# A two-layer decoder on one core: rotary tables of later batches made early and kept in DRAM, key preparation and query scaling at other places

## The chip, the core and the metric

The kernel runs on one core of a Trainium2 chip. The metric is device time in microseconds (us) of one execution. The core has five engines with in-order queues of their own: TensorE (PE in the profile, its weight loads PEld), VectorE (DVE), ScalarE (ACT), GpSimd (POOL) and SyncE (SP), which issues most of the DMAs here. L12 means line 12 of the kernel before.

## The reference

Four batches of 256 tokens, width 256, go through a decoder of two layers. Only the part around the change is shown in code; the rest is told in a sentence each.

```python
# layer 0: self-attention (16 heads, causal), attention over ctx (1601 tokens, masked), ternary feed-forward
x = x + _L0_attn_ref(_layernorm(x), ...)
x = x + _L0_xattn_ref(_layernorm(x), ctx_2048, mask)
x = x + _L0_ffn_ref(_layernorm(x), w_fc, w_proj)
# layer 1: gated recurrence, then the grouped attention that the change is about, then 8 experts, top 2
x = x + _L1_attn_ref(_layernorm(x), ...)
x = x + _L1_xattn_ref(_layernorm(x), ctx_2048, Wq, Wk, Wv, Wo, q_norm_w, k_norm_w, ctx_pos, tok_pos)
x = x + _L1_ffn_ref(_layernorm(x), w_gate, wi_0, wi_1, wo)

def _L1_xattn_ref(draft_hidden, context_hidden, ...):      # 16 query heads, 4 key heads, head size 128
    q = _rms_norm(draft_hidden @ Wq.T, q_norm_w)
    kv_in = concatenate([context_hidden, draft_hidden], axis=1)      # 1601 + 256 = 1857 keys
    k = _rms_norm(kv_in @ Wk.T, k_norm_w)
    v = kv_in @ Wv.T
    q, k = _rope(q, draft_pos), _rope(k, all_pos)      # x * cos(emb) + rotate_half(x) * sin(emb)
    probs = softmax(q @ k.T / sqrt(128))
    return (probs @ v) @ Wo.T
```

The positions differ from batch to batch, so the rotary tables are computed on the chip: angles (position times frequency, brought into the range of the Sin function), then cos and sin multiplied by the norm weights, for 1857 key positions (15 chunks of 128, `ctabk` and `stabk`, 128x1920 each) and for 256 query positions (`ctabq` and `stabq`, 128x256 each).

## The kernel before, in words

Everything is float32. The kernel has two parts that overlap a little.

**The front** (to about 525 us). Four generators, one for each batch, run the stages of layer 0 and the recurrence of layer 1 (`before`: `self_attention`, `memory_attention`, `feed_forward`, `recurrence`). A loop over ticks advances them in turn; batch b starts at tick `START[b]`. Beside them other generators are advanced as filler: `values_ahead` (the values of layer 1's attention, computed for whole batches and kept in DRAM, tiles `vah`, `vst`), `keys_ahead` (the unrotated keys of batch 3, kept in DRAM), `shared_weights` (the ternary weights, from tick `TERN`), and `before_head` (what the first head of the long stage needs, from tick `SIDE`). The order in which the program issues instructions on each engine is made by a scheduler from this order of emission; `behind` adds that a piece isn't placed ahead of what was emitted before it.

**The long stage** (about 525 to 1690 us): layer 1's attention. The 16 units of batch and key head are called heads here, each with 4 query heads in two pairs. `steps` runs over 8 steps for each pair. A step emits, in this order: the exponential of an older pair's score tile (subtraction of the maximum `bc` on VectorE, L1383; Exp on ScalarE, L1386; the running sum on POOL, L1398), one score tile of two key chunks (`bsc` on TensorE, L1361; its scaled copy on ScalarE, L1362; the running maximum `acc` on VectorE, L1366), and two key chunks of an older pair's weighted values (`bpo`, L1407). After a pair, `maximum` turns `acc` into `bc` by transposes (`tm`, `mq`, `bc`), and `finish` multiplies by the output weights (`bpw`, L1437).

Between these stand pieces for the next head, at places that are written out by hand: place 2s comes after the scores of step s and place 2s + 1 after its weighted values, so a place is half a step. `base` is the first place of the head before. Each piece is a generator with stops in it:

- `prep_q` (two for each head, j = 0, 1): projection `pq` (L1239), squares on ScalarE (L1189), products with the tables on VectorE (`ropeq`, `ropuq`, L1190 and L1191), their sum (L1196) and the root of the mean square (`rnq`, L1199) on POOL; stop; scaling of the four heads by it on ScalarE (L1203); stop; transposes `tpq` and the copy to `qTb`. The stops are `HB` and `HC` places after the projection.
- `prep_kv` (units 0 to 3, up to 4 key chunks each): load of the context (`cTk`), projection `pk` (L1290), the same rotation, its root `kn` (which later scales the scores' copies); stop; transposes `tpk` and the copy to `kTb` (L1303). Unit i makes key chunks 4i to 4i + 3; unit 0 holds the batch's own tokens too.
- `angles` (9 pieces) and `tables`, once for each batch, `tokens` (the layer norm of the batch's tokens: `normed_tokens` with a root by POOL's power, L272) and `experts` of the batch before (`mo`: another such root), all spread over the places.

The first call of `tiles(b, g)` for a head takes its buffers and issues the loads of its key weights and of the kept values `vb`. The score tiles and most other TensorE results go through one ring of PSUM banks (`p1`), so a result that is copied late holds a bank. Rotary tables have one buffer each.

```python
    QA, KA, HB, HC = (2, 6), (11, 13, 15, 17), 5, 8
            for f, when in ((prep_q, QA), (prep_kv, KA)):
                for i, o in enumerate(when):
                    gen = f(b, g, i)
                    spot = put(base + 2 * o, gen, bank=f is prep_q)
                    if f is prep_q:
                        put(spot + HB, gen)
                    put(spot + HC, gen, True, True)
```

Of the kernel before, what the change touches and what calls it, by code (L numbers as in the profile page):

```python
# [33 lines left out]
NROPE = 3  # L34
TERN = 34
SIDE = 48
KEPT = 3
# [79 lines left out]
def decoder_kernel(ctx: ExitStack, tc: tile.TileContext, at, t, out):  # L117
# [861 lines left out]
    def experts(b):  # L979
# [12 lines left out]
        yield  # L992
        r1 = rsqrt(mv[:, :, 1], 1e-5, f"mo{b}")
        yield
# [120 lines left out]
    def angles(b):  # L1115
# [3 lines left out]
        nc.sync.dma_start(out=pi, in_=t["pos"][b])  # L1119
        if b == 0:  # L1120
            V.tensor_scalar(knw, knw, math.sqrt(HD1), None, ALU.mult)
        pf = wk.tile([P, NCH], F32, tag="pf", name=f"pf{b}")
# [25 lines left out]
    def tables(b, only="kq"):  # L1148
# [3 lines left out]
        for nm, n, w in (("k", NCH, knw), ("q", 2, qnw)):  # L1152
# [13 lines left out]
            yield  # L1166

    def normed_tokens(b):
        mv = moments(xs[b], f"xb{b}")
        r1 = rsqrt(mv[:, :, 1], 1e-5, f"xb{b}")  # L1170
        bt[b]["centred"] = lambda: centred(fa(0, f"bxh{b}"), xs[b], mv, r1)
# [33 lines left out]
    def tiles(b, g):  # L1205

        if (b, g) not in gt:
            gt[b, g] = {

                "kT": odd("w3", f"kTb{b}{g}") if g % 2 else wk.tile([P, NKEY], F32, tag="kT", name=f"kTb{b}{g}"),  # L1210
                "v": (
                    odd("w4", f"vb{b}{g}")[:, 0 : NCH * HD1] if g % 2 else wk.tile([P, NCH * HD1], F32, tag="v", name=f"vb{b}{g}")
                ).rearrange("p (c d) -> p c d", c=NCH),
                "kn": sm([P, NCH], f"kn{g % 2}", f"kn{b}{g}", 1),
                "wkv": weight(
                    wk.tile([P, 512], F32, tag="wkv", name=f"wkv{b}{g}", bufs=2), "wkv1", 0, D, g * 256, (g + 1) * 256
                ),
            }
            for i in range(4):
                if (b, i) in kept_values:  # L1220
                    n, w = units(i)
                    r = min(P, w)
                    nc.sync.dma_start(
                        out=gt[b, g]["v"][0:r, 4 * i + 2 : 4 * i + 2 + n, :],
                        in_=kept_values[b, i][:, 0:r, g * HD1 : (g + 1) * HD1].rearrange("c p n -> p c n"),
                    )
        return gt[b, g]

    def prep_q(b, g, j):
# [75 lines left out]
    def before_head(b, g):  # L1305

        if g == 0:
            if b == 0:
                yield from angles(b)
            yield from tables(b)  # L1310
        late = None
        for i in (1, 2, 3):
# [141 lines left out]

    QA, KA, HB, HC = (2, 6), (11, 13, 15, 17), 5, 8
    DE, DW = 10, 11
# [36 lines left out]
    for k, (b, g) in enumerate(heads):  # L1493
        base = 32 * (k - 1)
        if k:
            if g == 0:
                gen = angles(b)
                for i in range(9):
                    put(base - 81 + 6 * i, gen, i == 8)
                gen = tokens(b)  # L1500
                for i, o in enumerate((-8, -6, -3)):
                    put(base + o, gen, i == 2, i == 2)
                for o, n in ((-5, "q"), (-3, "q"), (7, "k"), (11, "k")):
                    gen = tables(b, n) if o in (-5, 7) else gen
                    put(base + o, gen, o in (-3, 11))
            for f, when in ((prep_q, QA), (prep_kv, KA)):
                for i, o in enumerate(when):
                    gen = f(b, g, i)
                    spot = put(base + 2 * o, gen, bank=f is prep_q)
                    if f is prep_q:  # L1510
                        put(spot + HB, gen)
                    put(spot + HC, gen, True, True)
        gen = loader(b, g)
# [43 lines left out]
    tern = shared_weights()  # L1557
    keys = keys_ahead()
    gens = [before(b) for b in range(B)]
    work = steps()  # L1560
    through, tick, step, said = [False] * B, 0, 0, None
    while not all(through):
# [18 lines left out]
        if tick >= TERN:  # L1581
            behind(tern)
        if through[0] and psb:
            if said != "first":
# [85 lines left out]
```

## Time and profile before

| | us |
|---|---|
| median of 3 runs | 1748.08 |
| lowest and highest | 1747.93, 1750.08 |
| the profiled execution's own time | 1749.43 |
| its span, first to last instruction | 1747.4 |
| mean granted clock of TensorE | 0.993 |

| engine | busy us | share | instructions |
|---|---|---|---|
| PE | 1694.9 | 97% | 6642 |
| PEld | 971.5 | 56% | 6642 |
| DVE | 1302.7 | 75% | 2429 |
| ACT | 997.4 | 57% | 1742 |
| POOL | 877.5 | 50% | 719 |

The page is one execution, taken by the hardware profiler. Matmuls are pipelined and their ends are modelled, so a busy PE is not PE at its peak. A group is told by its line, engine, operation and tiles (out<-in) with its count, its busy time and the mean duration of one in ns; behind that stands the idle time of the engine just before it and what ended most of it. A list of waits names who waited for whom (total, times, longest). A timeline gives start, duration and, in brackets, the idle time before. A table of stretches gives the busy time of each engine between two times, the granted clock of TensorE, and what the DMAs moved.

### The profile page before, as it was taken

The numbers are of one execution on the slowest core, as the hardware profiler recorded it, in microseconds if no ns is written. First come the engines' busy times: TensorE is split into PE (matmuls) and PEld (weight loads), VectorE is DVE, ScalarE is ACT, GpSimd is POOL, SyncE is SP. The second block draws the span as 40 slices with busy tenths as digits, with TensorE's granted clock in tenths as the row PEclk, the third lists the DMA queues.
The fourth block names the chain that finished last, engine by engine and source line by source line (L and its number), as shares of the span: only waits on it lengthen the run. The fifth ranks groups of instructions, "written<-read, shape, count | busy, mean of one in ns | idle before, by whom it ended". The sixth has DMA issues, their size and how long they took to land.

```text
span 1747.4 us, 20643 instructions
## 1 busy us (share of the span) xinstructions
PE 1694.9 (97%) x6642; PEld 971.5 (56%) x6642; DVE 1302.7 (75%) x2429; ACT 997.4 (57%) x1742; POOL 877.5 (50%) x719
## 2 busy tenths in 40 slices
PE   8899989999999999999999999999999999999998
PEld 4455668765555455554555555555555555445546
DVE  6653476787668777787877878777877878788776
ACT  3456653656456656566665656556565656656551
POOL 2210032211126576676766756655665776676651
PEclk9999999999999999999999999999999999999999
DMA  7221334212231121121212121121222113011102
GB/s 258 99 90 50 90 99 128 75 66 90 97 109 46 38 82 35 55 58 31 89 32 70 47 67 52 55 82 35 73 61 67 51 37 93 26 37 48 43 0 67
DMA packets 113554, 119.10 MB, mean 68 GB/s; under 512 B 10000, under 2 KB 87332, under 8 KB 113448
## 3 DMA queue, kind: packets, MB, share of 16 engines
q1 hardware_dynamic: 111624, 116.39, 21.6%
q10 hardware_dynamic: 1824, 1.41, 0.3%
q8 instruction: 53, 0.87, 0.2%
q14 instruction: 53, 0.43, 0.1%
HBM read 100.20 MB, written 17.57 MB: 67 GB/s over the span
## 4 chain that ended last, share of the span: by engine, by line
PE 64%; DVE 12%; POOL 9%; ACT 9%; issue 4%; DMA 1%; POOLq 0%; DVEq 0%; ACTq 0%
PE bpo L1407 17%; PE bsc L1361 16%; PE pk L1290 5%; POOL sum L1398 5%; PE mph L1053 2%; PE bpw L1437 2%; PE vah L355 2%; ACT s L1386 2%; ACT s L1362 2%; DVE acc L1366 1%; PE xpo L740 1%; DVE s L1383 1%; PE pq L1239 1%; POOL ropeq L1196 1%; PE xsc L695 1%
## 5 line engine op out<-in xcount | busy, mean ns | idle before, releaser
L1398 POOL TENSOR_TENSOR sum<-sum,s 128x512 f32<-128x512 f32 (+1 forms) x411 | 536.7, 1306 | 84.1 <-ACT s L1386 59.0
L1361 PE MATMUL bsc<-qTb,kTb 128*128 128x512 f32 (+1 forms) x960 | 459.5, 599 | 6.8 <-ACT kTb L1303 6.7
L1407 PE MATMUL bpo<-s,vb 128*128 128x512 f32 (+1 forms) x960 | 459.9, 598 | 0.4 <-ACT s L1386 0.4
L1362 ACT ACTIVATE s<-bsc,kn 128x512 f32<-128x512 f32 (+1 forms) x480 | 316.5, 683 | 211.6 <-PE bsc L1361 194.6
L1366 DVE SCALAR_TENSOR_TENSOR acc<-bsc,kn,acc 128x512 f32<-128x512 f32 x448 | 333.0, 743 | 89.2 <-ACT s L1362 73.3
L1383 DVE TENSOR_TENSOR s<-s,bc 128x1024 f32<-128x1024 f32 (+1 forms) x256 | 289.4, 1142 | 14.7 <-PE bc L1379 14.5
L1386 ACT ACTIVATE s<-s 128x1024 f32<-128x1024 f32 (+1 forms) x256 | 256.5, 1006 | 53.8 <-DVE s L1383 52.2
L1361 PEld LDWEIGHTS bsc<-qTb,kTb 128*128 128x128 f32 (+1 forms) x960 | 174.2, 188 | 191.9 <-issue 135.3
L1407 PEld LDWEIGHTS bpo<-s,vb 128*128 128x128 f32 (+1 forms) x960 | 169.8, 191 | 141.7 <-issue 137.9
L1389 POOL TENSOR_TENSOR sum<-s 128x512 f32<-128x512 f32 x32 | 40.8, 1276 | 198.6 <-ACT s L1386 198.6
L1196 POOL TENSOR_TENSOR ropek<-ropek,ropuk 128x512 f32<-128x512 f32 (+1 forms) x64 | 78.2, 1222 | 123.7 <-DVE ropuk L1191 122.4
L1203 ACT ACTIVATE ropeq<-ropeq,rnq 128x128 f32<-128x128 f32 x128 | 41.2, 390 | 110.7 <-POOL rnq L1199 107.1
L355 PE MATMUL vah<-wv,vcT 128*128 128x512 f32 (+1 forms) x156 | 77.7, 633 | 5.1 <-DMA vcT<-in_ctxT 3.1
L1290 PEld LDWEIGHTS pk<-wkv,cTk 128*128 128x128 f32 x624 | 76.3, 192 | 8.3 <-issue 4.5
L1290 PE MATMUL pk<-wkv,cTk 128*128 128x128 f32 x624 | 77.4, 275 | 0.0
L1199 POOL TENSOR_TENSOR kn<-ssk,nhalf 128x4 f32<-128x4 f32 (+1 forms) x64 | 66.2, 1034 | 17.5 <-DVE ssk L1198 15.0
L1364 DVE TENSOR_SCALAR acc<-bsc,kn 128x512 f32<-128x512 f32 x32 | 24.0, 750 | 59.7 <-ACT s L1362 59.7
L1437 PEld LDWEIGHTS bpw<-wo,aT 128*128 128x128 f32 x256 | 48.5, 190 | 34.8 <-issue 21.1
L272 POOL TENSOR_TENSOR rsr_xa<-rse_xa,nhalf 128x2 f32<-128x2 f32 x4 | 3.4, 854 | 126.0 <-DVE rse_xa L270 126.0
L1437 PE MATMUL bpw<-wo,aT 128*128 128x256 f32 x256 | 65.6, 379 | 0.3 <-ACT aT L1413 0.3
L1196 POOL TENSOR_TENSOR ropeq<-ropeq,ropuq 128x512 f32<-128x512 f32 x32 | 43.8, 1368 | 40.2 <-PE bsc L1361 17.8
L358 ACT COPY vst<-vah 128x512 f32<-128x512 f32 (+1 forms) x52 | 30.2, 591 | 56.0 <-issue 18.3
(509 smaller groups left out, 2589.7 us busy)
## 6 DMA issues: line engine op xcount, KB each, us to landing
v<-vst SPq DMA_DIRECT2D x48, 256.0 KB
vb<-v SPq DMA_DIRECT2D x48, 256.0 KB
cTk<-in_ctxT SPq DMA_DIRECT2D x24, 512.0 KB
wq<-in_wq SPq DMA_DIRECT2D x16, 512.0 KB
wo<-in_wo SPq DMA_DIRECT2D x16, 512.0 KB
wi<-in_wi SPq DMA_DIRECT2D x32, 256.0 KB
xcT<-in_ctxT SPq DMA_DIRECT2D x12, 512.0 KB
xct<-in_ctx SPq DMA_DIRECT2D x12, 512.0 KB
```

Of the source, the lines that this page charges most:

```text
L355: T.matmul(pv[0:r, :], lhsT=cT[:, c, k * P : k * P + r], rhs=wv[c], start=c == 0, stop=c == 1)
L1196: G.tensor_tensor(r4, r4, u4[:, :, ::-1, :], ALU.add)
L1199: G.tensor_tensor(rn, ss[:, 0:n], nhalf[:, 0:n], ALU.pow)
L1290: T.matmul(pk[:, q, 0:w], lhsT=src, rhs=e["wkv"][:, c, 0:w], start=c == 0, stop=c == 1)
L1361: T.matmul(pc[0:n, :], lhsT=e["kT"][:, k * P : k * P + n], rhs=q, start=True, stop=True)
L1362: A.activation(s[0:n, i, :], pc[0:n, :], AF.Copy, scale=e["kn"][0:n, k : k + 1])
L1366: V.scalar_tensor_tensor(self.acc[0:n, :], pc[0:n, :], e["kn"][0:n, k : k + 1], self.acc[0:n, :], ALU.mult, ALU.max)
L1383: V.tensor_tensor(s[0:n, 0:w, :], s[0:n, 0:w, :], self.bc[0:n, None, :].to_broadcast([n, w, 512]), ALU.subtract)
L1386: A.activation(s[0:n, 0:w, :], s[0:n, 0:w, :], AF.Exp)
L1398: G.tensor_tensor(self.sum[0:n, :], self.sum[0:n, :], s[0:n, i, :], ALU.add)
L1407: T.matmul(self.po, lhsT=e["v"][0:n, k, :], rhs=self.s[c][0:n, i, :], start=k == 0, stop=k == NCH - 1)
L1437: T.matmul(pw[:, j * 256 : j * 256 + 256], lhsT=aT[:, o : o + P], rhs=e["wo"][:, self.h + h, :], start=True, stop=True)
```

## The change

What it does:

- `tables_ahead`, a new generator, makes the angles and tables of batches 1, 2 and 3 in the front, two pieces in each tick from tick 24 (`TABLES`), and writes them to DRAM. `load_tables` reads them back: the query tables 5 places before the head's base, the key tables 3 places after it. The pieces of `angles` and `tables` in the long stage go. Batch 0's tables stay as they were. The scaling of the key norm weights `knw` moves ahead of them.
- The key units of a head are prepared in the order 1, 2, 0, 3, at places 14, 18, 23 and 27 after the base (before: 0, 1, 2, 3 at 22, 26, 30, 34); transposes follow 8 places later, as before.
- The queries' scaling stands 8 places after the projection (before 5), their transposes 11 (before 8).
- The loads of the kept values leave `tiles` and get a place of their own, 22 after the base (`load_values`).
- `root` takes the place of POOL's power in `normed_tokens` of all batches and in `experts` of batches 0 to 2: VectorE adds the constant and runs `newton`, three steps from a bit pattern.

```diff
--- before.py
+++ after.py
@@ -33,6 +33,7 @@
 NDB = 3
 NROPE = 3
 TERN = 34
+TABLES = 24
 SIDE = 48
 KEPT = 3
 KEYS = (3,)
@@ -990,7 +991,7 @@
         iota = cc("iota8")[:, None, :].to_broadcast(s8)
         mv = moments(xb, f"mo{b}")
         yield
-        r1 = rsqrt(mv[:, :, 1], 1e-5, f"mo{b}")
+        r1 = rsqrt(mv[:, :, 1], 1e-5, f"mo{b}") if final else root(mv, f"mo{b}")
         yield
         xh = centred(ea(f"mxh{b}"), xb, mv, r1)
         yield
@@ -1117,8 +1118,6 @@
         d = bt.setdefault(b, {})
         pi = wk.tile([P, NCH], I32, tag="pi", name=f"pi{b}")
         nc.sync.dma_start(out=pi, in_=t["pos"][b])
-        if b == 0:
-            V.tensor_scalar(knw, knw, math.sqrt(HD1), None, ALU.mult)
         pf = wk.tile([P, NCH], F32, tag="pf", name=f"pf{b}")
         V.tensor_copy(pf, pi)
         sh = [P, NCH, 64]
@@ -1165,9 +1164,41 @@
             V.tensor_mul(stab[:, :, 0:64], sn[:, 0:n, :], wlo)
             yield
 
+    kept_tables = {}
+
+    def tables_ahead():
+
+        before = latest()
+        V.tensor_scalar(knw, knw, math.sqrt(HD1), None, ALU.mult)
+        keep_behind(before)
+        for b in range(1, B):
+            yield from angles(b)
+            yield from tables(b)
+            for nm, n in (("k", NCH), ("q", 2)):
+                kept_tables[b, nm] = []
+                for i, a in enumerate(bt[b][nm]):
+                    d = dram.tile([P, n * HD1], F32, tag=f"t{b}{nm}{i}", name=f"t{b}{nm}{i}")
+                    nc.sync.dma_start(out=d, in_=a.rearrange("p n d -> p (n d)"))
+                    kept_tables[b, nm].append(d)
+            yield
+
+    def load_tables(b, nm):
+
+        n = NCH if nm == "k" else 2
+        bt[b][nm] = tuple(wk.tile([P, n, HD1], F32, tag=f"{c}{nm}", name=f"{c}tab{nm}{b}") for c in "cs")
+        for a, d in zip(bt[b][nm], kept_tables[b, nm]):
+            nc.sync.dma_start(out=a.rearrange("p n d -> p (n d)"), in_=d)
+        yield
+
+    def root(mv, nm):
+
+        v = sm([P, 2], "rse2", f"rse_{nm}")
+        V.tensor_scalar(v, mv[:, :, 1], 1e-5, None, ALU.add)
+        return newton(v, nm, 2)
+
     def normed_tokens(b):
         mv = moments(xs[b], f"xb{b}")
-        r1 = rsqrt(mv[:, :, 1], 1e-5, f"xb{b}")
+        r1 = root(mv, f"xb{b}")
         bt[b]["centred"] = lambda: centred(fa(0, f"bxh{b}"), xs[b], mv, r1)
 
     def token_features(b):
@@ -1216,15 +1247,17 @@
                     wk.tile([P, 512], F32, tag="wkv", name=f"wkv{b}{g}", bufs=2), "wkv1", 0, D, g * 256, (g + 1) * 256
                 ),
             }
-            for i in range(4):
-                if (b, i) in kept_values:
-                    n, w = units(i)
-                    r = min(P, w)
-                    nc.sync.dma_start(
-                        out=gt[b, g]["v"][0:r, 4 * i + 2 : 4 * i + 2 + n, :],
-                        in_=kept_values[b, i][:, 0:r, g * HD1 : (g + 1) * HD1].rearrange("c p n -> p c n"),
-                    )
         return gt[b, g]
+
+    def load_values(b, g):
+        for i in range(4):
+            n, w = units(i)
+            r = min(P, w)
+            nc.sync.dma_start(
+                out=tiles(b, g)["v"][0:r, 4 * i + 2 : 4 * i + 2 + n, :],
+                in_=kept_values[b, i][:, 0:r, g * HD1 : (g + 1) * HD1].rearrange("c p n -> p c n"),
+            )
+        yield
 
     def prep_q(b, g, j):
         d, e = bt[b], tiles(b, g)
@@ -1308,6 +1341,7 @@
             if b == 0:
                 yield from angles(b)
             yield from tables(b)
+        run(load_values(b, g))
         late = None
         for i in (1, 2, 3):
             gen = prep_kv(b, g, i)
@@ -1452,7 +1486,7 @@
 
 
 
-    QA, KA, HB, HC = (2, 6), (11, 13, 15, 17), 5, 8
+    QA, KA, HB, HC, HQ = (2, 6), ((1, 14), (2, 18), (0, 23), (3, 27)), 8, 8, 11
     DE, DW = 10, 11
     places, taken = {}, set()
     STEPS = NPAIR * len(pairs) + DW + 5
@@ -1494,22 +1528,21 @@
         base = 32 * (k - 1)
         if k:
             if g == 0:
-                gen = angles(b)
-                for i in range(9):
-                    put(base - 81 + 6 * i, gen, i == 8)
                 gen = tokens(b)
                 for i, o in enumerate((-8, -6, -3)):
                     put(base + o, gen, i == 2, i == 2)
-                for o, n in ((-5, "q"), (-3, "q"), (7, "k"), (11, "k")):
-                    gen = tables(b, n) if o in (-5, 7) else gen
-                    put(base + o, gen, o in (-3, 11))
-            for f, when in ((prep_q, QA), (prep_kv, KA)):
-                for i, o in enumerate(when):
-                    gen = f(b, g, i)
-                    spot = put(base + 2 * o, gen, bank=f is prep_q)
-                    if f is prep_q:
-                        put(spot + HB, gen)
-                    put(spot + HC, gen, True, True)
+                put(base - 5, load_tables(b, "q"), True)
+                put(base + 3, load_tables(b, "k"), True)
+            for i, o in enumerate(QA):
+                gen = prep_q(b, g, i)
+                spot = put(base + 2 * o, gen, bank=True)
+                put(spot + HB, gen)
+                put(spot + HQ, gen, True, True)
+            for i, o in KA:
+                gen = prep_kv(b, g, i)
+                put(base + o, gen)
+                put(base + o + HC, gen, True, True)
+            put(base + 22, load_values(b, g), True)
         gen = loader(b, g)
         put(base + 60, gen, True)
     for b in range(B - 1):
@@ -1556,6 +1589,7 @@
     first_weights = {}
     tern = shared_weights()
     keys = keys_ahead()
+    turns = tables_ahead()
     gens = [before(b) for b in range(B)]
     work = steps()
     through, tick, step, said = [False] * B, 0, 0, None
@@ -1580,6 +1614,9 @@
             first_weights["wpj"] = fw("wpj", FF, D, nc.sync, "w4")
         if tick >= TERN:
             behind(tern)
+        if tick >= TABLES:
+            for _ in range(2):
+                behind(turns)
         if through[0] and psb:
             if said != "first":
                 said = next(first, "first")
```

## Prediction

> **What bounds the kernel now.** I read the page first, then TensorE's waits by stretch, then the engines' own timelines around the longest of them. The first line is the page's busy time, the next two are the table of busy time by stretch (PE, weight load, DVE, ACT, POOL, each with its count; then granted clock, DMA share, GB/s).
>
> ```profile
> PE 1694.9 (97%) x6642; PEld 971.5 (56%) x6642; DVE 1302.7 (75%) x2429; ACT 997.4 (57%) x1742; POOL 877.5 (50%) x719
> ...
> 147.00:262.00 115.00, 105.75 (x702) 73.17 (x701) 61.04 (x131) 69.69 (x177) 16.47 (x12) 1.00 0.27 79
> ...
> 525.00:1690.00 1165.00, 1145.45 (x4054) 618.54 (x4053) 930.07 (x1509) 702.93 (x1159) 768.89 (x617) 1.00 0.18 53
> ```
>
> TensorE is the bound: 98% of the long attention stage from 525 to 1690 us. The change takes no matmul away, so it can only give back TensorE's idle time. What ends that idle time in this stage, by the list of waits of TensorE in that window (total, times, longest):
>
> ```profile
> PE bc L1379 <- DVE mq L1375: 6.9, 3, 2.5
> PE bsc L1361 <- ACT kTb L1303: 6.7, 10, 1.2
> PE tpk L1301 <- DVE it L1060: 3.0, 5, 0.7
> PE tm L1373 <- DVE acc L1366: 2.3, 1, 2.3
> ```
>
> With two small ones (0.4 and 0.2) that is 19.5 us. The granted clock adds to it: after three of the four long gaps it is 0.66 over 5 us (table by stretch again):
>
> ```profile
> 755.00:760.00 5.00, 5.00 (x12) 2.25 (x11) 4.96 (x8) 1.37 (x2) 0.00 (x0) 0.66 0.00 0
> 1062.00:1067.00 5.00, 4.76 (x13) 2.86 (x13) 4.97 (x7) 1.35 (x2) 0.00 (x0) 0.66 0.00 0
> 1550.00:1555.00 5.00, 5.00 (x12) 2.22 (x11) 2.63 (x5) 1.00 (x2) 4.16 (x4) 0.66 0.09 26
> ```
>
> 0.34 of 5 us is 1.7 us, three times 5.1 us. So 19.5 + 5.1 = 24.6 us is all that the stage has to give.
>
> Where the long gaps come from shows in the timelines of DVE, POOL and ACT before the gap at 752 (start, us, what, idle time before it):
>
> ```profile
> 724.49 1.83 DVE L1161 TENSOR_TENSOR ctabk<-ang,knw 128x960 f32<-128x960 f32 x1
> ...
> 733.12 1.15 DVE L1164 SCALAR_TENSOR_TENSOR stabk<-sn,knw 128x960 f32<-128x960 f32 x1
> ...
> 734.85 1.56 DVE L1165 TENSOR_TENSOR stabk<-sn,knw 128x960 f32<-128x960 f32 x1
> ```
> ```profile
> 739.44 9.15 POOL L1398 TENSOR_TENSOR sum<-sum,s 128x512 f32<-128x512 f32 x6 [0.53 <-ACT s L1386]
> 748.55 1.26 POOL L1196 TENSOR_TENSOR ropeq<-ropeq,ropuq 128x512 f32<-128x512 f32 x1
> ```
> ```profile
> 750.82 1.28 ACT L1203 ACTIVATE ropeq<-ropeq,rnq 128x128 f32<-128x128 f32 x4 [6.07 <-POOL rnq L1199]
> ```
>
> The key tables hold VectorE back by 1.83 + 1.15 + 1.56 us. The subtractions of the pair then come in a bunch, so do the exponentials, and six additions stand in POOL's queue (9.15 us) ahead of the query's rotation. ScalarE has meanwhile reached the scaling of the queries (L1203) and waits 6.07 us for POOL's root, with the copies of the scores (L1362) queued behind it. VectorE's maximum needs those, `bc` needs the maximum, and TensorE stands. The gap at 1374 has the same chain; that at 1059 has an angle step in it as well; that at 1550 is a late `acc` behind batch 3's key preparation.
>
> **The change, part by part.**
>
> *Taken out of the attention stage.* Tables of three batches and angles of two: by VectorE's groups from 540 to 1690 us L1138 7.2, L1161 5.5, L1160 5.3, L1165 4.7, L1164 4.6, L1131 2.3, L1133 2.3, L1140 1.8, L1135 1.3, query tables 3.3, in all 38.3 us; on ScalarE two Sin, Abs, Sin triples (6.2 us) and four table loads of 1.28 us. Most of it is beside TensorE; its worth is the stalls that it causes.
>
> *Query scaling later.* The scaling now stands 8 half-steps after the projection, the transposes 11 (before: 5 and 8). A head of 16 steps takes some 73 us, so a half-step is 2.3 us and ScalarE meets L1203 about 6.8 us later. That is more than the 6.07 us that it waited at 744 to 751 and the 5.57 us at 1367 to 1373. Who is late next: the transposed queries, needed 32 half-steps after the base and now ready at about 23. With slack that long, I take the three `bc` waits as gone, 6.9 us, and of the clock the two stretches behind them, 3.4 us.
>
> *Keys sooner.* Units 1, 2, 0, 3 start at half-steps 14, 18, 23, 27 instead of 0, 1, 2, 3 at 22, 26, 30, 34, transposes 8 later as before. The last unit was transposed two scores ahead of its use; it now has some ten. Of the `kTb` waits (6.7 us) I keep 1.5 us, for unit 0, which still lands only at half-step 31 with its first use at 32: 5.2 us back. The rotations leave the end of the head, where `tm` waited for `acc`: 2.3 us and its clock, 1.7 us. In the changed order `tm` stands ahead of the next head's first score, with 2 `bpw`, 2 `bpo`, 4 `tpk` between: 0.86 + 0.86 + 1.72 + 0.44 = 3.9 us after the last score, against a lag of 2.6 us from that score to the end of its `acc` in the rows of undisturbed heads. It should not wait. Half of the `tpk` wait goes: 1.5 us. Together 6.9 + 3.4 + 5.2 + 2.3 + 1.7 + 1.5 = 21.0 us.
>
> *Roots on VectorE.* Five roots in this stage become 12 small VectorE instructions in place of one and a POOL power. At 858 us `rse_mo` to `nmr` took 1.38 us, of which VectorE idled 0.90; dependent small rows start 0.07 to 0.16 us apart, so the root costs 1 to 2 us. No gain, up to 1 us each. Small 128x2 rows beside POOL's additions take 0.75 and 1.01 us (L1029, L1032), so the bound above is 12 x 0.75 = 9 us on VectorE, with the next `acc` queued behind, so a TensorE gap of a few us each time. At 858 POOL took the power at once, so it was idle there, and I take the low end: 3 us in all, high end 12.
>
> Steady stage: 21 - 3 = 18 us back, between 8 and 24.
>
> *Loads.* Per batch two of 983 KB and two of 131 KB join SP's queue, with `wo` and the next `cTk` behind them. They wait for the last rotation of the old batch and have 11 half-steps, 25 us. At the 258 GB/s of the page's first slice they take 8.6 us: hidden. Without that cover each us late is a us of TensorE, three times. The value loads keep their order; their own place is nothing. The stores (6.7 MB) stand in SP's queue ahead of `xcT` loads at 194 to 213 us; those were issued some 6 us or more before their use. Nothing, up to 3 us.
>
> *Put into the front.* In the built order the three batches' work falls between 147 and 262 us. VectorE: per batch 0.16 + 1.14 + 0.65 + 0.65 + 3 x 1.15 + 0.65, tables 4 x 1.15 and 4 x 0.28, so 12.4 us, three times 37 us; it idles 115 - 61 = 54 us there. ScalarE: 3 x 3.1 us and eight table loads, 9.3 + 10.3 = 19.6 us, against 45 us idle. In sum it fits, but in lumps, and TensorE has only 9.2 us idle here. Lump by lump:
>
> ```profile
> 177.54 2.71 ACT L588 ACTIVATE sm<-sc,mx 128x128 f32<-128x128 f32 x8 [1.69 <-DVE mx L581]
> ```
>
> The first Sin lump (two loads, three activations, 5.66 us) falls just ahead of these exponentials, into 1.69 us of idle time: 4 us late, TensorE has some transposes meanwhile, so 3. VectorE from 187 to 201 gets 11.2 us against 6.6 us of gaps; the first transposes behind it had 3.5 us to spare: 1, and the second Sin lump 4.4 against 3.27 us: 1. From 225 to 250 VectorE is itself on the chain of waits (ternary weights, `xmq`, `kron`); 6.5 us join with some 2.5 us of gaps: 4. The last tables (5.7 us) meet 3.97 us of idle time, before a stretch in which TensorE waits for nothing: 0. Sum 9 us; least 2; most 18, with every lump late in full.
>
> *Two rules weighed.* The row on the clock: gaps of 2.3 to 2.5 us were enough for 3.4 us at half rate. [...] The row on table loads: at 347.45 a load takes 1.28 us and the Sin starts 0.01 us behind it. [...] I go by the rows in both.
>
> **Sum.** 9 - 18 = -9 us. The profiled execution took 1749.43 us (span 1747.4 and 2.0 around it), so 1740.4; the median of the three runs is 1748.08, 1.35 lower, so **1739 us**.
>
> **Rivals.**
> 1. *The front pays in full* (slower). One mechanism: the Sin lumps and the angle steps sit in the in-order queues of ScalarE and VectorE between 175 and 250 us, ahead of exponentials and maxima that TensorE's self-attention matmuls wait for. Price 18 us, while the attention stage returns 12 because new waits (roots, unit 0) take the place of some: +6, 1754 us. It decides once the stretch loses more than the stage returns. For it: TensorE is 92% busy there and the chain passes VectorE. Against: VectorE and ScalarE have 54 and 45 us of idle time.
> 2. *The stall changes its name* (no change). POOL's share is unchanged but for seven roots, ScalarE still meets a wait on it, only later, or `tm` and unit 0 wait at the head's turn: 9 returned, 9 paid, 1748 us. For it: 104 us of ScalarE's waits in the stage end on POOL's query root. Against: POOL sits idle at the start of nearly every pair.
> 3. *The front hides nearly all*: 2 paid, 21 returned, 1729 us.
>
> **How the numbers follow.** Forecast 0.60 (own range 1732 to 1745), rival 1 0.20, rival 2 0.13, rival 3 0.07. The bounds of 0.2% (3.5 us, about what a measurement can tell) are 1744.6 and 1751.6. Faster: 0.58 of the forecast's 0.60, rival 3, a little of rival 2: 0.66. Same: 0.15. Slower: most of rival 1: 0.19. The range reaches from rival 3 to rival 1, 1729 to 1754.
>
> **What would show it.** Right: no `bc` wait over 1 us behind `mq` in the attention stage, no granted clock below 0.9 in any 5 us stretch after 525, the `kTb` wait below 2 us, and the attention's first score some 9 us later than 509.5. Wrong: a first score over 16 us later, ACT waits on POOL's `rnq` that still reach 6 us, or a new wait of `tm` or of `bsc` at each head's turn.

## The result: slower by 0.8%, and the profile after

The changed kernel takes 1763.53 us (median of 10 runs, 1753.78 to 1767.57) against 1748.12 us for the kernel before (10 runs beside them, 1744.48 to 1751.16). The ratio is 1.0078, 95% interval [1.0061, 1.0096]. The forecast was 1739 us and its range ended at 1754: it was wrong, and on the wrong side. The profiled execution took 1764.92 us (span 1762.9, mean granted clock 0.982).

The page's busy times, then the scores' tile (the two times in us are its first and last start). Line numbers from here on are those of each run's own kernel.

```profile
PE 1706.4 (97%) x6642; PEld 984.2 (56%) x6642; DVE 1309.7 (74%) x2506; ACT 1000.2 (57%) x1745; POOL 858.5 (49%) x712
```
```profile
L1395 PE MATMUL bsc<-qTb,kTb x960: 590/592/874, 539.9 to 1700.9; 128*128 128x512 f32 x192
```

The same matmuls, 11.5 us more of TensorE's time. The first score comes at 539.9 us, before at 509.5: the front pays 30.4 us. From there to the end of the span it is 1223.0 us, before 1237.9: the attention stage gives 14.9 back. 30.4 - 14.9 = 15.5 us is the whole difference of the two spans.

Where the front pays shows in the table of busy time by stretch (PE, weight load, DVE, ACT, POOL; granted clock; DMA share, GB/s):

```profile
182.00:206.00 24.00, 23.05 (x82) 14.37 (x85) 8.45 (x12) 10.13 (x28) 0.00 (x0) 0.50 0.22 87
...
216.00:223.00 7.00, 5.85 (x16) 4.76 (x17) 2.18 (x5) 6.34 (x9) 0.00 (x0) 0.52 0.00 0
...
267.00:278.00 11.00, 7.94 (x36) 5.37 (x37) 9.73 (x13) 5.93 (x8) 6.57 (x5) 0.53 0.17 50
```

In the kernel before the clock is 1.00 in all of them, and the first of them holds 170 matmuls instead of 82. TensorE looks 96% busy from 182 to 206 us, at half its clock. Lost at most: 0.50 x 24 + 0.48 x 7 + 0.47 x 11 = 20.5 us. What comes ahead of the first stretch, on ScalarE and on TensorE (start, us, what; in brackets the idle time before it; the products `sc<-trib,identb`, which write a mask, are bfloat16, the others float32):

```profile
175.41 1.28 ACT L1141 ACT_TABLE_LOAD   x1
176.70 1.00 ACT L1141 ACTIVATE sn<-ang 128x960 f32<-128x960 f32 x1
...
177.87 1.01 ACT L1142 ACTIVATE ang<-ang 128x960 f32<-128x960 f32 x1
178.90 1.10 ACT L1143 ACTIVATE ang<-ang,hpi 128x960 f32<-128x960 f32 x1
180.02 1.28 ACT L589 ACT_TABLE_LOAD   x1
```
```profile
178.02 0.44 PE L623 MATMUL tb<-cst,sm 128*128 128x128 f32 x2 [1.04 <-ACT sm L619]
...
179.46 0.46 PE L309 MATMUL tp_a<-cst,a 128*128 128x128 f32 x2 [0.78 <-DVE a L628]
...
182.72 0.80 PE L571 MATMUL sc<-trib,identb 128*128 128x384 bf16 x2 [2.36 <-ACT sm L589]
...
202.04 3.78 PE L641 MATMUL pw<-wo,aT 128*128 128x256 f32 x8
```

The Sin lump stands in ScalarE's queue ahead of the exponentials `sm`, as the forecast said, and TensorE waits 1.04, 0.78 and 2.36 us. The clock falls at 182.2 us. It comes back at 206.1, after the dense products with `wo` and not before. The second stretch begins at 216.3 us, inside a longer wait:

```profile
217.15 0.48 PE L309 MATMUL tp_xa<-cst,xxh 128*128 128x128 f32 x1 [4.52 <-ACT xxh L301]
```

ScalarE makes `xxh` from VectorE's `nmr`, and that stands at 216.12 us behind three angle steps of 1.15 us each (at 211.99, 213.39 and 215.05). Ahead of the third stretch (from 267.5 us) TensorE waits 0.89 and 1.11 us for ScalarE's `pT`, and across its start 2.58 us for VectorE's `xs`.

The waits of TensorE in the attention stage (total, times, longest):

```profile
PE tm L1407 <- DVE acc L1400: 4.3, 3, 2.3
PE bpo L1441 <- ACT aT L1447: 2.8, 1, 2.8
PE bsc L1395 <- DVE acc L1400: 2.3, 2, 1.2
PE bsc L1395 <- DVE it L1061: 0.5, 1, 0.5
PE bpo L1441 <- ACT s L1420: 0.4, 1, 0.4
```

The waits of `bc`, of `kTb` and of `tpk` are gone: 10.3 us in place of 19.5, and other names.

### The profile page after: what moved, and what is told of

It is laid out like the page before. It is cut to its first block, busy times and chain, and to the rows that moved or that the text cites. A ratio compares the mean times of both kernels' runs of the same rounds, so it can differ in the third digit from the quotient of the medians.

```text
span 1762.9 us, 20717 instructions
## 1 busy us (share of the span) xinstructions
PE 1706.4 (97%) x6642; PEld 984.2 (56%) x6642; DVE 1309.7 (74%) x2506; ACT 1000.2 (57%) x1745; POOL 858.5 (49%) x712
## 5 line engine op out<-in xcount | busy, mean ns | idle before, releaser
L1432 POOL TENSOR_TENSOR sum<-sum,s 128x512 f32<-128x512 f32 (+1 forms) x411 | 527.6, 1284 | 61.4 <-ACT s L1420 36.6
L1417 DVE TENSOR_TENSOR s<-s,bc 128x1024 f32<-128x1024 f32 (+1 forms) x256 | 289.6, 1143 | 15.8 <-PE bc L1413 15.5
L1441 PEld LDWEIGHTS bpo<-s,vb 128*128 128x128 f32 (+1 forms) x960 | 174.3, 191 | 167.1 <-issue 156.7
L1336 ACT COPY kTb<-tpk 128x512 f32<-128x512 f32 (+1 forms) x64 | 35.1, 549 | 59.7 <-PE tpk L1334 59.7
## 6 DMA issues: line engine op xcount, KB each, us to landing
cTk<-in_ctxT SPq DMA_DIRECT2D x24, 512.0 KB
wq<-in_wq SPq DMA_DIRECT2D x16, 512.0 KB
wo<-in_wo SPq DMA_DIRECT2D x16, 512.0 KB
xcT<-in_ctxT SPq DMA_DIRECT2D x12, 512.0 KB
xct<-in_ctx SPq DMA_DIRECT2D x12, 512.0 KB
```

The costliest lines, as they stand in the source:

```text
L1417: V.tensor_tensor(s[0:n, 0:w, :], s[0:n, 0:w, :], self.bc[0:n, None, :].to_broadcast([n, w, 512]), ALU.subtract)
L1432: G.tensor_tensor(self.sum[0:n, :], self.sum[0:n, :], s[0:n, i, :], ALU.add)
L1441: T.matmul(self.po, lhsT=e["v"][0:n, k, :], rhs=self.s[c][0:n, i, :], start=k == 0, stop=k == NCH - 1)
```

## Experiments

Each run is set against runs of the kernel before on the same chip. "Stage" is the time from the first score to the end of the span of the profiled run.

| run | ratio to before, 95% interval | first score, us | stage, us |
|---|---|---|---|
| before | 1 | 509.5 | 1237.9 |
| changed kernel | 1.0078 [1.0061, 1.0096] | 539.9 | 1223.0 |
| tables in the stage again | 1.0015 [1.0005, 1.0026] | 513.5 | 1234.9 |
| tables in the front alone | 1.0066 [1.0046, 1.0086] | 535.6 | 1222.3 |
| changed, no activations | 1.0018 [1.0000, 1.0035] | 523.6 | 1223.1 |
| changed, no table loads | 1.0016 [1.0000, 1.0032] | 525.3 | 1221.2 |
| changed, 12 filler products | 1.0139 [1.0120, 1.0159] | 544.6 | 1223.0 |
| front alone, from tick 4 | 1.0044 [1.0028, 1.0061] | 531.1 | 1226.4 |
| front alone, from tick 8 | 1.0066 [1.0051, 1.0082] | 533.1 | 1222.4 |
| before, tables split | 1.0057 [1.0039, 1.0075] | 525.5 | 1234.0 |
| changed, filler at the first gap | 1.0063 [1.0042, 1.0085] | 535.5 | 1224.6 |
| keys and queries alone | 1.0009 [0.9996, 1.0022] | 510.1 | 1237.2 |
| queries alone | 1.0039 [1.0026, 1.0051] | 507.2 | 1240.3 |
| keys alone | 0.9911 [0.9896, 0.9926] | 513.9 | 1216.2 |
| changed, queries' places undone | 1.0042 [1.0028, 1.0055] | 537.4 | 1213.2 |
| keys alone, queries sooner | 0.9968 [0.9957, 0.9980] | 512.0 | 1228.7 |

### Which half pays, which half returns

Tables back in the stage:

```diff
...
-                put(base - 5, load_tables(b, "q"), True)
-                put(base + 3, load_tables(b, "k"), True)
+                gen = angles(b)
+                for i in range(9):
+                    put(base - 81 + 6 * i, gen, i == 8)
+                for o, n in ((-5, "q"), (-3, "q"), (7, "k"), (11, "k")):
+                    gen = tables(b, n) if o in (-5, 7) else gen
+                    put(base + o, gen, o in (-3, 11))
...
-        if tick >= TABLES:
-            for _ in range(2):
-                behind(turns)
```

> The changed kernel with one part undone: angles and tables of batches 1 to 3 are made in the attention stage again, at the places of the kernel before; order of the keys, places of the queries, values' load and roots stay changed. Theory A (the front's table work costs about 30 us, above all through TensorE's clock at half rate, and the new places return some 15 us in the stage): first score of the attention back at 509 to 511 us, no half-rate clock between 121 and 700 us, time 1732 to 1738. Theory B (the stage's return comes from the tables leaving it, the new places return nothing): 1746 to 1751. Theory C (the new order of keys and values shifts the front, not the tables): first score still over 530 us, time over 1755.

And the other way round, the kernel before with `tables_ahead` and `load_tables` and nothing else:

> The kernel before with one part of the change alone: tables of batches 1 to 3 made in the front from tick 24, kept in DRAM and loaded back; order of keys, places of the queries, values' load and roots as before. Theory A: the front's 30 us are paid (first score 537 to 542 us, TensorE at half rate for 20 us or more between 180 and 225 us), and the stage returns only the part of its stalls that the tables' lumps made, 5 to 10 us: 1768 to 1775. Theory B (the tables' leaving is what returns): 1760 to 1766, as the changed kernel. Theory C: first score near 510, time 1738 to 1748.

The first gave 1750.91 us, no half-rate stretch between 121 and 700 us, and a first score at 513.5. Theory A was right on the front's clock (its first score, 509 to 511, came out later), but the time is theory B's: the stage is only 3 us shorter. The second gave 1760.73 us, again as B asked: 26.1 us paid by the front, 15.6 returned by the stage, with none of the new places. Its waits in the stage:

```profile
PE bsc L1386 <- ACT kTb L1328: 6.0, 9, 1.0
PE tpk L1326 <- DVE it L1061: 3.3, 5, 0.7
PE tm L1398 <- DVE acc L1391: 0.8, 1, 0.8
```

`bc` is gone here although the queries are scaled where they were; `kTb` and `tpk` have stayed. The return of the tables' leaving is mainly the `bc` waits (6.9 us) and the clock, which fell three times for 3.4 us in the stage before and never falls in this one. The two parts add up on the front (4.0 + 26.1 = 30.1 of 30.4).

### What in the front is paid for

ScalarE's three activations for batches 1 to 3 left out, the rest as in the changed kernel:

```diff
-        A.activation(sn, ang, AF.Sin)
-        A.activation(ang, ang, AF.Abs)
-        A.activation(ang, ang, AF.Sin, bias=hpi, scale=-1.0)
+        if not b:
+            A.activation(sn, ang, AF.Sin)
...
```

> The changed kernel without ScalarE's three activations for the angles of batches 1 to 3 (their tables are then made of the angles, without cosine and sine); VectorE's work, stores and loads stay. Theory A (the lumps of table loads and Sin on ScalarE make TensorE wait in the self-attention, and that halves its clock): no half-rate stretch over 4 us between 175 and 225 us, first score at 515 to 522 us, time 1740 to 1747. Theory B (VectorE's angle and table work is what TensorE waits for): half-rate stretches stay, first score at 535 us or later, time 1758 to 1764. Theory C (stores and queues): as B.

The activations kept, with Identity in place of Sin:

> The changed kernel with Identity in place of Sin in the front for batches 1 to 3 (their tables are then no cosines and sines): three activations for each batch stay, 9.3 us in all, the eight loads of function tables, 10.3 us, go. Theory A: a lump is 3.1 us and not 5.7, TensorE's waits behind it are shorter and the clock stays full for most of the stretch: first score at 517 to 527 us, time 1742 to 1752. Rival (any insertion of three activations ahead of the exponentials halves the clock): half-rate stretch of over 15 us behind 180 us stays, first score over 535 us, time over 1757.

Medians 1749.44 and 1749.77 us; first scores 16.3 and 14.6 us earlier than in the changed kernel. The second lies within theory A's ranges, the first misses them by 2 us in time and in first score; both lie 7 to 11 us from the rivals. The stretches at half clock from 182 to 206 and 216 to 223 us are gone in the first; in the second 3.4 us of half clock are left at 213 us. So the switches of the function table (eight loads) are nearly all of ScalarE's share: the activations' own 9.3 us show as 1.7 us of the first score. Both traces are of executions with a mean clock of 0.991; four of the twelve executions of each ran at 0.983 to 0.986 and took 1754 to 1760 us, and where the clock fell in those isn't known. Over all executions the means are 1761.3 us for the changed kernel, 1751.4 and 1751.5 for these two: 10 us apart, less than the medians. One stretch stays in both, here in the run without activations:

```profile
251.00:262.00 11.00, 8.36 (x37) 5.73 (x38) 10.90 (x15) 2.36 (x5) 6.14 (x5) 0.53 0.16 48
```

VectorE is 10.90 of 11 us busy in it, and across its start TensorE waits 2.6 us for VectorE's `xs`. I put this one down to VectorE's queue, which the angles and tables have pushed back; no run took VectorE's part away alone.

### Is it the clock or the waits?

Work was added to test this. First four products behind each Sin:

```diff
+        if b:
+            fill = p1(f"fill{b}")
+            for i in range(4):
+                T.matmul(fill, lhsT=ident, rhs=sn.rearrange("p a b -> p (a b)")[:, 0:512], start=True, stop=True)
```

> The changed kernel with work added: four 128x512 products of TensorE behind the first Sin of each of batches 1 to 3 in the front, 12 in all, 0.59 us each at full clock, 7 us of pure extra work whose result nobody reads. Theory A (some 2.5 us of idle time in one 3.4 us stretch halves TensorE's clock, and the half rate from 182 to 206 us, not the waits themselves, is the largest part of the front's price): the half-rate stretch behind 182 us goes or is below 7 us, the first score comes 4 to 12 us earlier than the changed kernel's 539.9, time 1751 to 1760 although work was added. Rival (the waits are the price, the clock follows from them): time 1765 to 1771, first score at 543 us or later.

1770.76 us, in the rival's range, but this run doesn't decide: the products waited for the sines themselves (11.4 us, one of them 10.3 us at 263), and a product is two entries, so 24 of them, 0.46 us each in a row: 11 us of work and not 7. In spite of all that the first score moved only 4.7 us: the half-rate stretch behind the first lump was 7 us long and not 24.

```profile
185.00:192.00 7.00, 6.61 (x28) 3.79 (x28) 2.33 (x5) 3.72 (x11) 0.00 (x0) 0.51 0.13 40
192.00:212.00 20.00, 15.52 (x130) 9.93 (x129) 16.62 (x35) 12.89 (x37) 0.70 (x1) 1.00 0.46 167
```

Here the clock was back at 191.9 us, in the middle of the same score products and transposes and ahead of the dense `pw`. So it was done again with one group of three, behind `tb`, which leaves every other instruction of TensorE in its order:

> The changed kernel, every queue of TensorE in the same order, and three 128x512 products on the sine of batch 1 put in at one place: between tb (178.0 us in the changed kernel's trace) and tp_a, where TensorE stands idle for most of 178 to 182.7 us. Their result is read by nobody. A product shows as two entries, 0.46 us each in a row, so 2.8 us of added work in a gap of some 3.4 us; what waits for ScalarE waits as before. Theory A (the idle share of one 3.4 us stretch halves the clock, and that costs 12 us by 206 us): the half-rate stretch from 182 to 206 us goes or shrinks below 7 us, first score 8 to 13 us earlier than 539.9, median 1751 to 1757. Rival (the waits cost, the clock only follows): half rate or not, first score within 2 us of 539.9 or later, median 1763 to 1767.

TensorE's timeline, and the table of stretches:

```profile
176.91 2.74 PE L1180 MATMUL fill<-sn,cst 128*128 128x512 f32 x6
...
186.30 0.49 PE L571 MATMUL sc<-trib,identb 128*128 128x384 bf16 x2 [1.32 <-ACT sm L589]
...
197.53 3.78 PE L641 MATMUL pw<-wo,aT 128*128 128x256 f32 x8
```
```profile
187.00:202.00 15.00, 15.00 (x64) 10.00 (x62) 5.74 (x8) 5.15 (x13) 0.00 (x0) 0.54 0.32 133
```

With 2.7 us of useless work added, the first score of the profiled run comes 4.4 us earlier. Of that 1.4 us stands ahead of the filler already (`tb` starts at 176.64 us, there at 178.02; the changed kernel's trace is at half rate for 17.1 us ahead of it, this one for 10.2); 3.1 us are gained between `tb` and `pw`. The clock now falls 5.6 us later, at 187.8, and comes back at 201.5, again at the dense `pw`: some 14 us at half rate instead of 24. That speaks against the rival. Theory A's own numbers were missed as well: the stretch wasn't below 7 us, the first score not 8 to 13 us earlier, and the median, 1758.73 us, lies between the two theories; its ratio's interval overlaps that of the changed kernel (means of all executions 1757.7 and 1761.3). The fall was put off, not prevented, and the time alone decides nothing.

The traces say more when the time up to the first score is split into TensorE's busy and idle time. The number of matmuls up to there is the same in all (2319 or 2320 entries, 2326 with the filler), so more busy time for them is a slower clock. Each row is one execution, that of the changed kernel one of its slower six:

| run | first score, us | busy, us | idle, us | at half rate, us |
|---|---|---|---|---|
| before | 509.5 | 482.3 | 27.2 | 13.7 |
| changed kernel | 539.9 | 499.4 | 40.5 | 58.0 |
| tables in the front alone | 535.6 | 498.4 | 37.2 | 54.6 |
| changed, no activations | 523.6 | 485.8 | 37.8 | 23.9 |
| changed, no table loads | 525.3 | 486.6 | 38.7 | 27.3 |
| changed, filler at the first gap | 535.5 | 496.0, 2.7 of it the filler | 39.5 | 41.0 |

The changed kernel's 30.4 us are 17.1 us of longer busy time and 13.3 us of idle time. Without the table loads 12.8 us of the busy time go and only 1.8 of the idle time: in these executions what the loads cost is the clock, and hardly the waits themselves. So the clock is shown as the larger part of the front's price, at the first gap by added work and over the whole front by this split. What each of the other two stretches costs alone is inferred from their rows.

### Does the place in the front matter?

> The kernel before with the tables of batches 1 to 3 made in the front, as in the run with the tables alone in the front, but from tick 4 in place of 24: in the built order the three Sin lumps stand near 40, 88 and 130 us instead of 175, 217 and some 265. Theory A (the price is that of the place: exponentials and maxima of the self-attention of several batches, with small matmuls on TensorE): first score 515 to 525 us in place of 535.6, time 1738 to 1750. Rival (28 us of VectorE and 20 us of ScalarE join full queues wherever they stand): first score 530 us or later, time 1755 or more.

> As the run from tick 4, but from tick 8: the Sin lumps stand near 67, 117 and 300 us. Theory A: two lumps lie ahead of the crowded self-attention stretch and one behind it, so no half-rate clock between 175 and 225 us, first score 514 to 524 us, time 1736 to 1749. Rival as there: first score 530 us or later, time 1755 or more.

Both edits change one constant (`TABLES`) in the kernel with the tables alone in the front. 1754.92 and 1758.28 us, first scores at 531.1 and 533.1: theory A was wrong here and the rival right. The first score came 4.5 and 2.5 us earlier than from tick 24, no more, and TensorE fell to half clock at other places (five stretches between 48 and 226 us from tick 4, before the change two).

### What the stage had to give

The key tables of the kernel before in 8 pieces of four chunks at places 3 to 17:

> The kernel before, its tables still in the attention stage, but the key tables made in 8 pieces of up to four chunks at 8 places two half-steps apart, instead of 2 pieces of all 15 chunks. Theory D (what the tables cost in the stage is their lumps on VectorE, 1.8 + 1.2 + 1.6 us in a row, which bunch the additions on POOL and make the queries' root late): the three waits of bc (6.9 us) and the half-rate clock behind them (5 us) go, time 1736 to 1742. Rival (it is the sum of the tables' work, 38 us of VectorE): the waits stay in another place, time 1746 to 1751. Second rival (four times the instructions cost more than they save): over 1752.

1758.14 us, in the second rival's range, and the run answers only half: batch 0's tables are split too, which moves its first head, and the first score comes 16 us later. In the stage the three `bc` waits are still there (6.6 us in total), so smaller lumps of the tables alone don't take them away.

Then the new places without the tables, and each of the two alone:

> The changed kernel with the tables in the attention stage and the roots on POOL, both as before: what is left of the change is the order and places of the keys, the later scaling and transposes of the queries and the values' own place. Against the run with the tables in the stage it tells the price of the roots. If the roots are what moved its first score from 509.5 to 513.5 us: first score 509 to 511 us, time 1744 to 1748. If the new places did that: first score 513 us or later, time 1749 to 1752.

> The kernel before with one part of the change alone: the queries' scaling 8 places after the projection and the transposes 11 after (before 5 and 8). Tables, keys, values' load and roots as before. By the prediction's step (bc waits 6.9 us and 3.4 us of clock behind them go): first score 509 to 511 us, no bc wait over 1 us in the attention stage, time 1736 to 1741. Rival (the stall changes its name: with the tables' work still on VectorE, something else is late at the same heads): the bc waits go, waits of equal size on acc, kTb or aT come, time 1744 to 1750.

> The kernel before with one part of the change alone: keys in the order 1, 2, 0, 3 at 14, 18, 23, 27 half-steps after the base and the values' load in its own place. Tables in the stage, queries' places and roots as before. By the prediction's step (kTb 5.2, tpk 1.5, tm 2.3 and its clock 1.7 us back): kTb wait below 2 us, time 1736 to 1741. Rival (the keys' rotations now fall beside the queries' or the maxima): kTb waits go, but waits of tm, bpo on aT or bsc on acc and on VectorE's rotations come, 8 to 16 us in all, time 1745 to 1752.

Together they give nothing that can be told from no change (1748.75 us). The first score at 510.1 also bounds the price of the roots on VectorE: 3.4 us of the front (513.5 with them), of which 1.6 is a wait of the tokens' transposes `tp_xb` that only kernels with the new roots have. The rest isn't sure: the run with the keys alone has the old roots and its first score at 513.9, where the clock is at half rate for 17.1 us up to there and not for 10.2, and TensorE's busy time is 3.3 us longer. Apart, the two parts pull against each other. The queries' later places alone make 1752.94 us, above the rival's range too. The `bc` waits fall from 6.9 to 2.4 us, and the stall changes its name:

```profile
PE tm L1373 <- DVE acc L1366: 12.3, 8, 3.5
PE bsc L1361 <- ACT kTb L1303: 4.9, 8, 0.9
PE tpk L1301 <- DVE it L1060: 2.6, 4, 0.7
PE bc L1379 <- DVE mq L1375: 2.4, 2, 1.4
```

The keys' order alone makes **1731.19 us, ratio 0.9911 [0.9896, 0.9926]**: the best version of all, 5 us below the range that the prediction's step gave. All waits of its stage above 0.5 us:

```profile
PE bpo L1443 <- ACT aT L1449: 2.5, 3, 1.6
PE tm L1409 <- DVE acc L1402: 1.6, 2, 0.8
PE bsc L1397 <- DVE acc L1402: 1.6, 2, 0.8
PE mpe L1067 <- DVE it L1061: 1.4, 1, 1.4
PE tpk L1336 <- POOL ropek L1229: 0.9, 1, 0.9
```

No `bc`, no `kTb`, and the clock never falls in the stage: 21.7 us shorter than before, with all tables still made in it.

Then the changed kernel with only the queries put back, and the keys alone with the queries' transposes still sooner (6 places after the projection). The edit of the first:

```diff
-                put(spot + HB, gen)
-                put(spot + HQ, gen, True, True)
+                put(spot + 5, gen)
+                put(spot + 8, gen, True, True)
```

> The changed kernel with one part undone: the queries' scaling and transposes at 5 and 8 places after the projection, as before the change. Theory F (the later transposes stand just ahead of a pair's last scores and delay its maximum, with or without the tables in the stage): the waits of tm on acc and of bpo on aT, 10.3 us in the changed kernel's stage, fall below 6 us, stage from first score to the end 1214 to 1219 us in place of 1223, median 1755 to 1760; the rest, some 10 us over the kernel before, is the front's price. Rival (the cost exists only beside the tables' work): median 1762 to 1766.

> The run with the keys sooner alone, and the queries' transposes 6 places after the projection in place of 8. Theory F (what counts is the distance to the end of the pair): no cost, 1728 to 1733, as the keys alone. Rival (the transposes then meet rotations that aren't done, and TensorE waits for ScalarE): waits of tpq of 5 us or more, 1735 to 1742.

1753.97 us: theory F, a little better than asked for. The stage falls from 1223.0 to 1213.2 us, its waits on `acc` and `aT` from 9.4 to 4.1 (the 10.3 us in the expectation are all five waits), and the clock stays full in it up to its last microsecond. So the queries' later places cost some 10 us of the changed kernel. With the tables still in the stage they cost as well: 21.0 us of the stage beside the keys' new order (1216.2 to 1237.2), 2.4 beside the old one (1237.9 to 1240.3). The second run gave 1742.43 us: sooner costs some 10 us too, with `tm` waiting 7.6 us and a score 3.1 us for `it`. That is neither theory F nor its rival, whose wait of `tpq` didn't come. Of the three places tried, 6, 8 and 11 half-steps behind the projection, 8 is the best; distance to the pair's end is not the whole of it.

## Why the prediction was wrong

**The front, 9 us, is the step that failed.** It measured 30.4 us; the tables alone cost 26.1, the roots 1.6 to 3.4. The direct waits were sized about right: with the tables alone TensorE idles 10.0 us longer up to the first score. The missing term is the clock: its busy time for the same matmuls grows by 16.1 us. The forecast had the row for it (gaps of 2.3 to 2.5 us gave 3.4 us at half rate) and used it to count what the stage gives back, but put no such term on the waits that it made itself in the front. Sized by that row it would have been three times 1.7 us; the runs showed 24, 7 and 10 us at half rate. The VectorE lump from 225 to 250 us (4 us) and the last tables (0) were also judged by idle time, where a stretch with the clock at 0.53 came.

**The stage, 18 us, measured 14.9 (9.3 of idle time, 5.6 of busy time), and is right in the sum only.** Of its terms:

- *Query scaling later (10.3 us)* failed. The forecast took a later place in the program for a later place in ScalarE's queue. In the traces the scaling hardly moved: its first instruction starts 9.8 us after the start of the projection before (median of 28) and 8.9 after, and 8.9 as well in the changed kernel with the queries' places undone; in all three it starts 0.03 us behind the root that it waits for. Only the transposes moved, from 18.1 to 25.5 us behind the start of the projection. ScalarE's wait, before and after:

```profile
ACT ropeq L1203 <- POOL rnq L1199: 103.2, 28, 6.5
```
```profile
ACT ropeq L1234 <- POOL rnq L1230: 114.0, 29, 6.8
```

 The forecast had named this as a sign of being wrong ("ACT waits on POOL's `rnq` that still reach 6 us"). The `bc` waits did go, but the tables' leaving alone takes them away, and so does the keys' order alone; the queries' places alone left 2.4 us of them and put 12.3 us of `tm` beside.
- *Keys sooner (10.7 us)* was too small: 21.7 us from the first score on, 17.3 of the whole span. It removed the `bc` waits too, which the forecast had given to the queries.
- *`tm` not waiting* failed: 4.3 us in three waits. With the queries' places undone no wait of `tm` is listed.
- *Roots (3 us in the stage)*: the run with them has no longer stage than the one without (1234.9 and 1237.2); what shows of their cost, the 1.6 us wait of `tp_xb`, was in the front, where the forecast had nothing.
- *Loads and stores: nothing* held. None of the five kinds of wait that TensorE has left in the stage ends on a DMA.

**The rivals.** The first had the sign and the place (the Sin lumps between 175 and 250 us) with a price of 18 us; it was 30, 17 of them longer busy time at half clock, so even the top of the range was passed. Its second half (new waits, less returned) came in part. Of the forecast's signs of being right, the `bc` and `kTb` waits did go; but the clock was 0.66 from 1387 to 1392 and from 1544 to 1549 us, and of the signs of being wrong the late first score and `rnq` at 6.8 us came, and new waits of `tm` and `bsc` too, though not at each head's turn.

**The two rows.** On the clock: the longest wait ahead of the fall at 182.2 us was 2.36 us, and 1.32 us ahead of the one at 187.8 in the run with the filler at the first gap. So the row (gaps of 2.3 to 2.5 us were enough) was right to go by, and not strong enough. Theory A's figure in the runs with filler, some 2.5 us of idle time in one 3.4 us stretch, fits the first of these falls (from 178.8 to 182.2 us TensorE is busy for 0.90 of 3.4 us) and not the second. Of the front's three falls only that at 216.3 us came in a longer wait, 3.7 us into one of 4.52. The clock came back at 206.1 and 201.5 us, right behind 3.78 us of dense `pw`, with 20 and 10 us of transposes and narrow products at half rate ahead of that. But in the run with 12 filler products it came back among the same instructions, 6.8 us after its fall. What brings it back is not shown, and no run here tells transposes and the narrow 32-row products apart. On table loads: the one at 175.41 us took 1.28 us, and Sin started 0.01 us behind it, as in the row.

## What to carry to other kernels

Work that is moved into "idle" time of another engine is paid for by the engine that waits for it (26.1 us up to the first score here, with the tables alone). Where that one was TensorE in a stretch of transposes and narrow products, three waits of 0.8 to 2.4 us were followed by 24 us at half clock, and one of 1.3 us by 14: add a clock term to every new wait, and reckon that it can last until the next dense products, as in these two runs; in a third it ended ahead of them, after 7 us. Look in each engine's order of instructions for whether a step moves before giving it a price: the scaling's new place moved it by less than 1 us, and the transposes that went along with it by 7. When a change has several parts, run them one by one: this one held a gain of 0.9% (the keys) inside a loss of 0.8%.

## What the runs showed of the hardware that was not expected

- TensorE's clock fell at 182.2 us after three waits, none longer than 2.4 us, and stayed at half for 24 us while the profile showed it 96% busy. In the run with the filler at the first gap it fell behind a wait of 1.3 us.
- In the traces of the two kernels the half-rate stretches that end inside the span last 3.41, 6.83, 10.24 and 23.89 us, each a whole multiple of the first; in the run with the filler at the first gap one lasts 13.7.
- The ten runs of the changed kernel fall into two groups that follow the mean granted clock: six at 0.981 to 0.984 take 1763.14 to 1767.57 us, four at 0.988 to 0.990 take 1753.78 to 1756.59. The means are 9.5 us apart; the clocks (0.9822 and 0.9890) times the span differ by 12 us. The kernel before shows no such step, but variants with work in the front spread in the same way: without table loads 1746.09 to 1750.26 us at 0.989 to 0.992, 1755.36 and 1755.87 at 0.986, 1758.60 and 1759.22 at 0.984. A median of theirs depends on how many executions of each kind it holds. What decides between the groups from run to run stays open, as does why the later transposes delay the maxima.
